# Layer 2's second linear map by seven products of half blocks for groups 4 to 12

## The chip, the cores and the metric

The kernel runs on one core of a Trainium2 chip. Its time is the device time of one execution in microseconds (us). The engines are called by the profile's names: PE is TensorE (PEld its weight loads), DVE is VectorE, ACT is ScalarE, POOL is GpSimd, SP the engine that issues most DMAs. L1089 is line 1089 of the kernel before the change.

## What is computed

Four graph layers run one after the other on x (128 batches of 64 nodes, 256 features, all float32). Each takes a layer norm and a ReLU of x, applies a network with the 64 x 64 adjacency, and adds the result to x. The third of them, called layer 2, is the one that matters here:

```
h   = max(layernorm(x), 0)
agg = A_hat @ h                                     # per batch, over the nodes
h   = relu(batchnorm(agg @ W1.T + b1, g1, be1))     # 256 -> 512
out = batchnorm(h @ W2.T + b2, g2, be2)             # 512 -> 256
x   = x + out
```

The batch norms take mean and variance over all 8192 tokens (batches times nodes), so no value of `out` can be finished before the whole linear map W2 is done. Layer 3 follows with three more linear maps, of which the first takes layer 2's `out`.

## The kernel before

**Groups and buffers.** The 8192 tokens are worked on in 16 groups (NG) of 512 (GN). Inside layer 2 features lie on the partitions: a group's hidden activations are a tile h1s[g] of 128 x 4 x 512, with the 512 hidden features as four chunks of 128, and its output `o` is 128 x 2 x 512. Such tiles are called arenas (L738) and come from three places: ar_right holds eight, ar_left seven, keep one. h1s[0] to h1s[7] lie in ar_right, h1s[8] in keep, the rest in ar_left. The outputs, two groups to an arena, take the arenas of ar_right that the first groups give back. PSUM has eight banks of 128 x 512, handed out in turn (L49).

**The stretch around the change.** The first linear map (hidden_products and hidden_out, L760 to L781) writes h1s and takes a bn_stats of each chunk. bn_finish (L1003) makes scale and shift of the batch norm of it: for each chunk a bn_aggr, an addition, a power on POOL (L1013), and DVE steps of one column (L1016, L1019, L1020). L1016 forms -(mean + bias). For this linear map's norm and the next one's the statistics are taken of the products in PSUM, without the bias, so the bias has to be added to the mean; the stored values have it added as they leave PSUM (L778, and L1098 for the second map).

The loop of L1076 does the second linear map. For each group: four ACT activations in place (L1079: ReLU with the norm's scale and shift), eight matmuls of 128 x 128 weights against 128 x 512 activations (L1089: four chunks of the contraction for each of two output chunks), then for both output chunks a bn_stats (L1103, DVE) and an eviction to `o` with the bias (L1098, ACT). The weights w1 (L949) and w2 (L950) of the two maps are two halves of one tile.

After group 12 (L1106) layer3_weights (L1048) brings layer 3's weights by DMA on SP into arenas that h1s[8] to h1s[11] have given back, and forms sums and differences of their blocks on POOL (L1063 to L1071); some of these go into w1 (L1070). Behind the loop stands bn_finish for the second norm (L1108) and first_start (L1156), the turn into layer 3: normalize, transpose back, add to x, and the first group's layer norm.

**Seven products.** Elsewhere the kernel already multiplies matrices of 2 x 2 blocks with seven products in place of eight (L164 to L237). `sums` forms four combinations of the left matrix's blocks, `differences` four of the right one's, t1 to t4. `seven` issues products 1, 5, 6 and 7 into four banks; ACT copies 1 and 5 out (L173, L174), DVE adds 6 and 7 to these copies (L176, L177). Its function `finish` then has POOL add the two for the block (1, 1) (L180), lets product 2 accumulate on product 1 (block (0, 0), evicted by ACT, L224), product 3 on product 5 and product 4 on product 7 (blocks (0, 1) and (1, 0), added by DVE, L185 and L189). In layer 3 it is used at L1220, L1256 and L1301.

**What sets the order.** The instructions are traced in program order; a planner at compile time then gives each engine its own list, taking by program order what is ready by its own cost estimates, and puts semaphores where an instruction needs another engine's result or a buffer that is still read. Two instructions wait for each other only where the elements that they touch overlap. `tc.issue_after(ins)` keeps a block's instructions behind `ins` on its engine.

Of the kernel before, what the change touches and what calls it, by code (L numbers as in the profile page):

```python
# [9 lines left out]
AF = mybir.ActivationFunctionType  # L10
ALU = mybir.AluOpType
# [3 lines left out]
P = 128  # L15
# [5 lines left out]
NG = NTOK // GN  # L21
# [11 lines left out]
V_B2, V_G2, V_BE2 = 12, 14, 16  # L33
# [5 lines left out]
def adj_preln_kernel(ctx: ExitStack, tc: tile.TileContext, x_in, adj, vec, bg0, bg1,  # L39
                     wg0, wg1, wih, whh, wqkv, w1t, w2t, l3w1, l3w2, l3w3, out):  # L40
    nc = tc.nc
# [7 lines left out]
    def bank(shape=(P, 512)):  # L49
        return psp.tile(list(shape), F32, tag="ps", name="ps")  # L50
# [25 lines left out]
    vecs = const.tile([P, V_N], F32, tag="vecs", name="vecs")  # L76
# [85 lines left out]
    HN = GN // 2  # L162

    def seven(products, banks, p1, p5, out, end, parts=lambda b: [b]):  # L164

        ps = banks  # L170
        for i, p in zip((1, 5, 6, 7), ps):
            products[i](p, True)
        nc.scalar.copy(p1, ps[0])  # L173
        nc.scalar.copy(p5, ps[1])  # L174

        nc.vector.tensor_tensor(p1, p1, ps[2], ALU.add)  # L176
        added = nc.vector.tensor_tensor(p5, p5, ps[3], ALU.add)  # L177

        def finish():
            nc.gpsimd.tensor_tensor(out=out[1][1], in0=p1, in1=p5, op=ALU.add)  # L180
            end(1, 1, None)
            products[2](ps[0], False)
            end(0, 0, ps[0])
            products[3](ps[1], False)
            nc.vector.tensor_tensor(out[0][1], p1, ps[1], ALU.add)  # L185
            end(0, 1, None)
            products[4](ps[3], False)
            for to, p, q in zip(*(parts(b) for b in (out[1][0], p1, ps[3]))):
                last = nc.vector.tensor_tensor(to, p, q, ALU.add)  # L189
                end(1, 0, None, to)  # L190
            return last.ins

        finish.behind = added.ins
        return finish

    def each_behind(behind, i):
        return tc.issue_after(behind[i].ins) if behind else nullcontext()
# [10 lines left out]
    def sums(eng, a11, a12, a21, a22, s1, s2, s3, s4, behind=None):  # L208

        ops = (  # L210
            (s1, a21, a22, ALU.add), (s2, s1, a11, ALU.subtract),
            (s3, a11, a21, ALU.subtract), (s4, a12, s2, ALU.subtract),
        )
        for i, (s, p, q, op) in enumerate(ops):
            with each_behind(behind, i):
                last = eng.tensor_tensor(out=s, in0=p, in1=q, op=op)
        return last.ins

    def ends_in(out, func):


        def end(m, n, ps, part=None):
            if ps is not None:
                nc.scalar.activation(out[m][n], ps, func)  # L224
            elif func != AF.Copy:
                o = out[m][n] if part is None else part
                nc.scalar.activation(o, o, func)  # L227

        return end

    def sevens(w, b, issue):


        (a11, a12), (_, a22), (s1, s2, s3, s4) = w
        (b11, _), (b21, b22), (t1, t2, t3, t4) = b
        pairs = ((a11, b11), (a12, b21), (s4, b22), (a22, t4), (s1, t1), (s2, t2), (s3, t3))
        return {i + 1: issue(*p) for i, p in enumerate(pairs)}  # L237
# [41 lines left out]
    with tc.tile_pool(name="lw", bufs=5) as lw:  # L279
# [6 lines left out]
        with tc.tile_pool(name="gw", bufs=1) as gw, tc.tile_pool(name="gcn", bufs=2) as gp, \  # L286
# [85 lines left out]
            for i, w_d in enumerate((wg0, wg1)):  # L372
                w = gw.tile([P, 2, D], F32, tag=f"wg{i}", name=f"wg{i}")
# [126 lines left out]
        with tc.tile_pool(name="back", bufs=1, reuse_waits="tile") as back_pool, \  # L500
# [188 lines left out]
            for p, nk in ((1, 8), (2, 8), (3, 7), (4, 8)):  # L689
                n = nk * HB  # L690
# [47 lines left out]
    def arena(pool):  # L738
        return pool.tile([P, 4, GN], F32, tag="arena", name="arena")
# [4 lines left out]
    st2 = bp.tile([P, 2, NG, 6], F32, tag="st2", name="st2")  # L744
    h1s = []
# [38 lines left out]
    with tc.tile_pool(name="att", bufs=2, reuse_waits="tile") as ap_:  # L784
# [103 lines left out]
        def attend(eT, v):  # L888
            pss = [bank((P, 2 * GT, NODES)) for _ in range(2)]
            for t in range(GT):  # L890
                for m in range(2):
                    for b in range(2):
                        for par in range(2):
                            rows = slice(par * 64, par * 64 + 64)
                            nc.tensor.matmul(
                                pss[par][b * 64 : b * 64 + 64, 2 * t + m, :],
                                lhsT=eT[rows, 2 * t + m, b * 64 : b * 64 + 64],
                                rhs=v[rows, 2 * t + b, m * 64 : m * 64 + 64],
                                start=True, stop=True,
                            )  # L900
            return pss
# [20 lines left out]
        for g in range(NG):  # L922
            if g == NG - NK + 1:
                hres_pool.__exit__(None, None, None)
                with tc.using_default_side("right"):
                    ar_right = ctx.enter_context(
                        tc.tile_pool(name="arena_r", bufs=NG // 2, reuse_waits="tile")
                    )
            hT_all, blocks = hT
# [5 lines left out]
            q, k, finish = queries_keys(blocks)  # L935
# [11 lines left out]
            if g == NG - 1:  # L947

                w1 = w_att[:, :, 0:512]  # L949
                w2 = w_att[:, :, 512:1024].rearrange("p a (b f) -> a p b f", f=D)  # L950
# [8 lines left out]
            if last is not None:  # L959
                pss = attend(eT, v_last)  # L960
# [22 lines left out]
        with tc.issue_after(sub):  # L983
# [4 lines left out]
            rstd, nmr, _ = ln_scale(xs[2], lambda: add_output(NG - 2, pss, ri))  # L988
# [6 lines left out]
        pss = attend(eT, v_last)  # L995
# [4 lines left out]
    ar_left = ctx.enter_context(tc.tile_pool(name="arena_l", bufs=NG // 2 - 1, reuse_waits="tile"))  # L1000
    outs = []

    def bn_finish(st, n, v_0, v_g, v_b, tag):  # L1003


        scs, shs = [], []
        for m in range(n):
            mv = bp.tile([P, 2], F32, tag=f"{tag}mv{m}", name=f"{tag}mv{m}")
            sc = bp.tile([P, 1], F32, tag=f"{tag}sc{m}", name=f"{tag}sc{m}")
            sh = bp.tile([P, 1], F32, tag=f"{tag}sh{m}", name=f"{tag}sh{m}")  # L1010
            nc.vector.bn_aggr(mv, st[:, m].rearrange("p g s -> p (g s)"))
            nc.vector.tensor_scalar(sc, mv[:, 1:2], BN_EPS, None, ALU.add)
            nc.gpsimd.tensor_tensor(out=sc, in0=sc, in1=mhalf[:, 0:1], op=ALU.pow)  # L1013
            mean = mv[:, 0:1]

            nc.vector.tensor_scalar(  # L1016
                mean, mean, vecs[:, v_0 + m : v_0 + m + 1], -1.0, ALU.add, ALU.mult
            )
            nc.vector.tensor_tensor(sc, sc, vecs[:, v_g + m : v_g + m + 1], ALU.mult)  # L1019
            nc.vector.scalar_tensor_tensor(  # L1020
                sh, mean, sc, vecs[:, v_b + m : v_b + m + 1], ALU.mult, ALU.add
            )
            scs.append(sc)
            shs.append(sh)
        return scs, shs
# [47 lines left out]

    sc1, sh1 = bn_finish(st1, 4, V_B1, V_G1, V_BE1, "n1")

    for g in range(NG):  # L1076
        a = h1s[g]
        for m in range(4):
            nc.scalar.activation(  # L1079
                a[:, m, :], a[:, m, :], AF.Relu,  # L1080
                bias=sh1[m], scale=sc1[m],
            )
        pss = [bank() for _ in range(2)]
        order = [(c, m) for c in range(4) for m in range(2)]
        if g == NG - 1:

            order.sort(key=lambda cm: cm[1])
        for c, m in order:
            nc.tensor.matmul(  # L1089
                pss[m], lhsT=w2[c // 2][:, c % 2, m * P : (m + 1) * P], rhs=a[:, c, :],  # L1090
                start=(c == 0), stop=(c == 3),
            )

        if g % 2 == 0:
            outs.append(arena(ar_right))
        o = outs[-1][:, 2 * (g % 2) : 2 * (g % 2) + 2, :]
        def evicted(m):
            nc.scalar.activation(  # L1098
                o[:, m, :], pss[m], AF.Identity, bias=vecs[:, V_B2 + m : V_B2 + m + 1]
            )  # L1100

        for m in range(2):
            nc.vector.bn_stats(st2[:, m, g, :], pss[m])  # L1103
            if (g, m) != (NG - 1, 1):
                evicted(m)
        if g == NG - 4:  # L1106
            w_three = layer3_weights()
    sc2, sh2 = bn_finish(st2, 2, V_B2, V_G2, V_BE2, "n2")  # L1108

    b1, t1s, a2, s2s, b3, t3s = w_three  # L1110

# [44 lines left out]
    def first_start():  # L1156
# [26 lines left out]
        for g in range(1, 3):  # L1183
            normalize(g, chunks=[1], on_scalar=range(2))
        evicted(1)
        lns = []
        for k in range(2):
# [141 lines left out]
    def finish(g, pss):  # L1329
        if g == NG - 1:  # L1330

            for k in range(2):
                for q, queue in enumerate((nc.sync, nc.scalar)):
                    t = 2 * k + q
                    xt = xs[g][:, t, :]
                    nc.vector.tensor_tensor(xt, xt, pss[q][:, k, :], ALU.add)
                    queue.dma_start(out=out_view[:, g * GT + t, :], in_=xt)
            return
        for q in range(2):
            xq = xs[g].rearrange("p (k q) d -> p q k d", q=2)[:, q]  # L1340
            nc.vector.tensor_tensor(xq, xq, pss[q], ALU.add)
        nc.sync.dma_start(out=out_view[:, g * GT : (g + 1) * GT, :], in_=xs[g])
# [18 lines left out]
    a, finish_start = first_start()  # L1361
    s3 = None
    for g in range(NG + 1):
# [10 lines left out]
        if s3 is not None:  # L1374
            pss = [bank((P, 2, D)) for _ in range(2)]
# [13 lines left out]
        if g < NG:  # L1389
# [6 lines left out]
            if g + 1 < NG:  # L1396
                a = start(g + 1, behind)
# [53 lines left out]
```

## Time and profile before

| | us |
|---|---|
| median of 3 runs | 2474.28 (2473.75 to 2474.61) |
| the profiled execution | 2476.59 |
| its span in the trace | 2474.8 |
| PE busy in the span | 2454.1 |
| the loop of L1076 (1577.6 to 1688.6) | 111.0 |
| PE busy in it | 110.5 |
| DVE, ACT, POOL busy in it | 26.8, 65.6, 21.6 |

Times in the views are counted from the span's start. A line of groups gives the source line, engine and operation, what it writes and reads by the program's tile names, the shape and the count; behind the bar its busy time in us, the mean of one in ns, and the idle time of the engine just before it with what ended most of that. In a timeline the first two numbers are start and duration in us, and the square bracket holds the wait before. A float32 matmul stands as two records. [...]

### The profile page before, as it was taken

The page shows a single profiled execution, that of the slowest core. Times are in us where ns is not written, and L with a number is a line of the kernel's source. Part 1 is how long each engine was busy: PE and PEld are TensorE (multiplying, and loading weights), DVE is VectorE, ACT ScalarE, POOL GpSimd, SP SyncE. Part 2 cuts the span into 40 slices and gives each one's busy share as a digit, 9 for nine tenths or more (in the row PEclk, how much of TensorE's full clock was granted, in tenths as well). Part 3 has the DMA queues.
Part 4 walks back from the last instruction along what each step waited for, and adds up shares of the span by engine and source line. Part 5 has one row for each costly group of instructions (what it writes and reads, how often), then busy time and mean ns, then how long its engine had stood idle before and what let it go on. Part 6 is the DMA issues. An engine that isn't in the chain of part 4 may idle for free.

```text
span 2474.8 us, 46316 instructions
## 1 busy us (share of the span) xinstructions
PE 2454.1 (99%) x19646; PEld 2073.2 (84%) x19646; DVE 1512.6 (61%) x2705; ACT 1145.7 (46%) x2032; POOL 439.8 (18%) x368
## 2 busy tenths in 40 slices
PE   9999999999999999999999999999999999999999
PEld 7678888889999998888888864446998898898888
DVE  6758866666566565566599986425555455454544
ACT  4557754444454443444565566754333323333332
POOL 4432211111111111121133331013011111101110
PEclk9999999999999999999999999999999999999999
DMA  3200000000000000000122110010000000000000
GB/s 126 93 2 1 1 18 1 1 1 34 1 1 1 1 1 1 1 13 1 39 73 71 46 35 1 1 60 1 10 10 18 10 10 16 12 10 10 18 10 18
DMA packets 48558, 48.00 MB, mean 19 GB/s; under 512 B 3680, under 2 KB 44768, under 8 KB 48352
## 3 DMA queue, kind: packets, MB, share of 16 engines
q1 hardware_dynamic: 47360, 44.23, 5.8%
q8 instruction: 154, 2.52, 0.4%
q10 hardware_dynamic: 992, 0.82, 0.1%
q14 instruction: 52, 0.43, 0.1%
HBM read 28.26 MB, written 8.39 MB: 15 GB/s over the span
## 4 chain that ended last, share of the span: by engine, by line
PE 89%; DVE 6%; ACT 2%; issue 1%; POOL 1%; DMA 0%; SPq 0%; ACTq 0%; DVEq 0%; POOLq 0%
PE ps L533 41%; PE ps L1256 16%; PE ps L1301 8%; PE ps L1089 4%; PE ps L766 4%; PE ps L144 4%; PE ps L1220 3%; PE ps L476 2%; PE ps L452 2%; PE ps L799 2%; PE ps L821 1%; ACT arena L227 1%; POOL arena L180 1%; PE ps L882 1%; DVE st L92 0%
## 5 line engine op out<-in xcount | busy, mean ns | idle before, releaser
L533 PE MATMUL ps<-diff,s 128*128 128x256 f32 (+1 forms) x1824 | 393.5, 371 | 0.9 <-DVE diff L653 0.9
L1256 PE MATMUL ps<-arena 128*128 128x256 f32 x1792 | 392.4, 381 | 0.0
L1256 PEld LDWEIGHTS ps<-arena 128*128 128x128 f32 x1792 | 337.9, 190 | 54.0 <-issue 9.3
L533 PEld LDWEIGHTS ps<-diff,s 128*128 128x128 f32 x1824 | 345.9, 190 | 33.8 <-issue 1.6
L547 ACT ACTIVATE gates<-gates,lbias 128x512 f32<-128x512 f32 (+5 forms) x426 | 244.2, 620 | 203.2 <-DVE gates L185 147.3
L180 POOL TENSOR_TENSOR gates<-p 128x512 f32<-128x512 f32 (+1 forms) x115 | 149.6, 1301 | 878.7 <-DVE p L177 827.9
L533 PE MATMUL ps<-h,w 128*128 128x256 f32 (+1 forms) x1028 | 241.0, 371 | 0.0
L533 PE MATMUL ps<-diff,w 128*128 128x256 f32 (+1 forms) x1040 | 238.7, 370 | 0.0
L533 PEld LDWEIGHTS ps<-diff,w 128*128 128x128 f32 x1040 | 197.4, 190 | 18.2
L533 PEld LDWEIGHTS ps<-h,w 128*128 128x128 f32 x1028 | 194.7, 190 | 19.0 <-issue 0.5
L547 ACT ACTIVATE gates<-ps,lbias 128x256 f32<-128x256 f32 (+3 forms) x213 | 91.6, 476 | 247.0 <-PE ps L533 246.9
L227 ACT ACTIVATE arena<-arena 128x512 f32<-128x512 f32 (+1 forms) x160 | 88.6, 582 | 193.4 <-POOL arena L180 101.5
L180 POOL TENSOR_TENSOR arena<-arena 128x512 f32<-128x512 f32 x64 | 73.2, 1143 | 528.4 <-DVE arena L177 528.4
L1301 PE MATMUL ps<-arena 128*128 128x128 f32 x1280 | 149.7, 276 | 0.0
L185 DVE TENSOR_TENSOR gates<-p,ps 128x512 f32<-128x512 f32 (+1 forms) x115 | 76.4, 664 | 119.5 <-PE ps L533 119.4
L1301 PEld LDWEIGHTS ps<-arena 128*128 128x128 f32 x1280 | 145.5, 192 | 1.1
L96 POOL TENSOR_TENSOR rstd<-rstd,mhalf 128x4 f32<-128x4 f32 (+1 forms) x66 | 66.1, 1002 | 425.5 <-DVE rstd L95 418.8
L185 DVE TENSOR_TENSOR arena<-arena,ps 128x512 f32<-128x512 f32 x64 | 39.7, 621 | 152.5 <-PE ps L1256 87.4
L533 PE MATMUL ps<-state,w 128*128 128x256 f32 (+1 forms) x512 | 116.1, 370 | 0.9 <-ACT p L173 0.8
L176 DVE TENSOR_TENSOR p<-p,ps 128x512 f32<-128x512 f32 (+1 forms) x131 | 86.7, 661 | 48.9 <-PE ps L533 48.2
L533 PE MATMUL ps<-state,s 128*128 128x256 f32 (+1 forms) x512 | 115.8, 369 | 0.0
L189 DVE TENSOR_TENSOR gates<-p,ps 128x512 f32<-128x512 f32 (+1 forms) x115 | 76.7, 667 | 63.9 <-PE ps L533 63.2
(185 smaller groups left out, 4063.2 us busy)
## 6 DMA issues: line engine op xcount, KB each, us to landing
x<-in_x SPq DMA_DIRECT2D x27, 512.0 KB, 4.1
v<-vt SPq DMA_DIRECT2D x128, 64.0 KB, 2.1
out<-x SPq DMA_DIRECT2D x15, 512.0 KB, 2.9
w<-in_wih SPq DMA_DIRECT2D x4, 1024.0 KB, 7.5
w<-in_whh SPq DMA_DIRECT2D x3, 1024.0 KB, 4.8
arena<-in_l3w SPq DMA_DIRECT2D x3, 1024.0 KB, 5.2
w<-in_wqkv SPq DMA_DIRECT2D x1, 768.0 KB, 4.4
x<-in_x SPq DMA_DIRECT2D x2, 256.0 KB, 3.2
```

The costliest lines, as they stand in the source:

```text
L144: last = nc.tensor.matmul(pss[b][half * 64 : half * 64 + 64, c, t, :], lhsT=src[rows, t, col : col + 64], rhs=a2[rows, :], start=True, sto ...
L176: nc.vector.tensor_tensor(p1, p1, ps[2], ALU.add)
L180: nc.gpsimd.tensor_tensor(out=out[1][1], in0=p1, in1=p5, op=ALU.add)
L185: nc.vector.tensor_tensor(out[0][1], p1, ps[1], ALU.add)
L189: last = nc.vector.tensor_tensor(to, p, q, ALU.add)
L227: nc.scalar.activation(o, o, func)
L533: nc.tensor.matmul(ps[:, r], lhsT=wc[:, j, :], rhs=bc, start=first and r == 0 and c == 0, stop=True, skip_group_check=True,)
L547: nc.scalar.activation(o, ps, func, bias=lbias[:, col : col + 1])
L766: nc.tensor.matmul(ps, lhsT=w1[:, c, m * P : (m + 1) * P], rhs=a[:, 2 + c, :], start=(c == 0), stop=(c == 1),)
L1089: nc.tensor.matmul(pss[m], lhsT=w2[c // 2][:, c % 2, m * P : (m + 1) * P], rhs=a[:, c, :], start=(c == 0), stop=(c == 3),)
L1256: nc.tensor.matmul(ps[:, r, :], lhsT=w[:, c, col : col + P], rhs=b[:, c, :], start=first and r == 0 and c == 0, stop=c == 1, skip_group_ch ...
L1301: nc.tensor.matmul(ps[:, t, :], lhsT=w[:, c, t * P : (t + 1) * P], rhs=b[:, c, :], start=first and t == 0 and c == 0, stop=c == 3, skip_gr ...
```

## The change

For groups 4 to 12 (SEVEN_FC2) the second linear map is done by `seven`. The left matrix is W2 as 2 x 2 blocks (output chunk m by halves c of the hidden features), the right one the activations as 2 x 2 blocks (halves of the hidden features by halves of the tokens). Each product has 256 tokens and two chunks of contraction. The four sums of weight blocks are made once, on POOL, in w1, which is free by then. The four differences of the activations (128 x 2 x 256 each) go, for each group anew, into one more arena of ar_right, tt, by DVE; the group's activations for this purpose are called for one group ahead. Three of the differences of group g + 1 stand between the first four products of group g and its `finish`, the fourth behind it. Products 1 and 5 are copied into a block of h1s[g] that no product reads. The statistics of these groups read `o` in SBUF, not PSUM.

Groups 0 to 3 and 13 to 15 keep their eight matmuls. All groups now store `o` without the bias b2, and the second norm gets it through its shift: with `biased=False` bn_finish adds the bias to -(mean + bias) again, so that the shift is that of values without it. The diff:

```diff
--- before.py
+++ after.py
@@ -1000,7 +1000,7 @@
     ar_left = ctx.enter_context(tc.tile_pool(name="arena_l", bufs=NG // 2 - 1, reuse_waits="tile"))
     outs = []
 
-    def bn_finish(st, n, v_0, v_g, v_b, tag):
+    def bn_finish(st, n, v_0, v_g, v_b, tag, biased=True):
 
 
         scs, shs = [], []
@@ -1016,6 +1016,8 @@
             nc.vector.tensor_scalar(
                 mean, mean, vecs[:, v_0 + m : v_0 + m + 1], -1.0, ALU.add, ALU.mult
             )
+            if not biased:
+                nc.vector.tensor_tensor(mean, mean, vecs[:, v_0 + m : v_0 + m + 1], ALU.add)
             nc.vector.tensor_tensor(sc, sc, vecs[:, v_g + m : v_g + m + 1], ALU.mult)
             nc.vector.scalar_tensor_tensor(
                 sh, mean, sc, vecs[:, v_b + m : v_b + m + 1], ALU.mult, ALU.add
@@ -1073,39 +1075,101 @@
 
     sc1, sh1 = bn_finish(st1, 4, V_B1, V_G1, V_BE1, "n1")
 
-    for g in range(NG):
+
+
+    SEVEN_FC2 = range(4, NG - 3)
+    fc2_a = [[w2[c][:, :, m * P : (m + 1) * P] for c in range(2)] for m in range(2)]
+
+    fc2_s = [w1[:, :, i * P : (i + 1) * P] for i in range(4)]
+    sums(nc.gpsimd, *fc2_a[0], *fc2_a[1], *fc2_s)
+
+    def fc2_blocks(a):
+        return [
+            [a[:, 2 * c : 2 * c + 2, n * HN : (n + 1) * HN] for n in range(2)] for c in range(2)
+        ]
+
+    def fc2_differences(a, which=range(4)):
+        (b11, b12), (b21, b22) = fc2_blocks(a)
+        t1, t2, t3, t4 = ts
+        ops = ((t1, b12, b11), (t3, b22, b12), (t2, b22, t1), (t4, b21, t2))
+        for i in which:
+            t, p, q = ops[i]
+            nc.vector.tensor_tensor(t, p, q, ALU.subtract)
+
+    def second_linear(a, o):
+
+
+        def product(w, b):
+            def issue(ps, first):
+                for c in range(2):
+                    nc.tensor.matmul(
+                        ps, lhsT=w[:, c, :], rhs=b[:, c, :], start=first and c == 0, stop=c == 1,
+                        skip_group_check=True,
+                    )
+
+            return issue
+
+        blocks = [[o[:, m, n * HN : (n + 1) * HN] for n in range(2)] for m in range(2)]
+        return seven(
+            sevens((*fc2_a, fc2_s), (*fc2_blocks(a), ts), product), [bank((P, HN)) for _ in range(4)],
+            a[:, 0, HN:], a[:, 1, HN:], blocks, ends_in(blocks, AF.Copy),
+        )
+
+    def activate(g):
         a = h1s[g]
         for m in range(4):
             nc.scalar.activation(
                 a[:, m, :], a[:, m, :], AF.Relu,
                 bias=sh1[m], scale=sc1[m],
             )
-        pss = [bank() for _ in range(2)]
-        order = [(c, m) for c in range(4) for m in range(2)]
-        if g == NG - 1:
-
-            order.sort(key=lambda cm: cm[1])
-        for c, m in order:
-            nc.tensor.matmul(
-                pss[m], lhsT=w2[c // 2][:, c % 2, m * P : (m + 1) * P], rhs=a[:, c, :],
-                start=(c == 0), stop=(c == 3),
-            )
+
+    for g in range(NG):
+        a = h1s[g]
+        if g not in SEVEN_FC2:
+            activate(g)
 
         if g % 2 == 0:
             outs.append(arena(ar_right))
         o = outs[-1][:, 2 * (g % 2) : 2 * (g % 2) + 2, :]
-        def evicted(m):
-            nc.scalar.activation(
-                o[:, m, :], pss[m], AF.Identity, bias=vecs[:, V_B2 + m : V_B2 + m + 1]
-            )
-
-        for m in range(2):
-            nc.vector.bn_stats(st2[:, m, g, :], pss[m])
-            if (g, m) != (NG - 1, 1):
-                evicted(m)
+        if g + 1 == SEVEN_FC2[0]:
+            tt = arena(ar_right).rearrange("p i (c n) -> p i c n", c=2)
+            ts = [tt[:, i] for i in range(4)]
+        ahead = g + 1 in SEVEN_FC2
+        if ahead:
+            activate(g + 1)
+        if g in SEVEN_FC2:
+            finish = second_linear(a, o)
+            if ahead:
+                fc2_differences(h1s[g + 1], range(3))
+            finish()
+            if ahead:
+                fc2_differences(h1s[g + 1], [3])
+            for m in range(2):
+                nc.vector.bn_stats(st2[:, m, g, :], o[:, m, :])
+        else:
+            pss = [bank() for _ in range(2)]
+            order = [(c, m) for c in range(4) for m in range(2)]
+            if g == NG - 1:
+
+                order.sort(key=lambda cm: cm[1])
+            for c, m in order:
+                nc.tensor.matmul(
+                    pss[m], lhsT=w2[c // 2][:, c % 2, m * P : (m + 1) * P], rhs=a[:, c, :],
+                    start=(c == 0), stop=(c == 3),
+                )
+
+            def evicted(m):
+                nc.scalar.copy(o[:, m, :], pss[m])
+
+            for m in range(2):
+                nc.vector.bn_stats(st2[:, m, g, :], pss[m])
+                if (g, m) != (NG - 1, 1):
+                    evicted(m)
+            if ahead:
+                fc2_differences(h1s[g + 1])
         if g == NG - 4:
             w_three = layer3_weights()
-    sc2, sh2 = bn_finish(st2, 2, V_B2, V_G2, V_BE2, "n2")
+    sc2, sh2 = bn_finish(st2, 2, V_B2, V_G2, V_BE2, "n2", biased=False)
 
     b1, t1s, a2, s2s, b3, t3s = w_three
 
```

## The prediction

> **What bounds the kernel now.** I read the page first, then the busy time by stage, the groups of instructions inside the stage that is changed, the chain of work that ended last, and the timelines of VectorE and GpSimd. The page's engine shares:
>
> ```profile
> PE 2454.1 (99%) x19646; PEld 2073.2 (84%) x19646; DVE 1512.6 (61%) x2705; ACT 1145.7 (46%) x2032; POOL 439.8 (18%) x368
> ```
>
> TensorE (PE) is busy nearly all the span, but that is an average; the changed loop has to be read by itself. Its groups, from 1577 to 1692 us:
>
> ```profile
> L1089 PE MATMUL ps<-arena,w 128*128 128x512 f32 x256 | 110.5, 593 | 0.5 <-ACT arena L1079 0.5
> ...
> L1079 ACT ACTIVATE arena<-arena,n1sh,n1sc 128x512 f32<-128x512 f32 x62 | 45.2, 819 | 1.9 <-DVE n1sh L1020 1.9
> L1103 DVE BATCH_NORM_STATS2 st<-ps 128x6 f32<-128x512 f32 x32 | 22.4, 698 | 82.4 <-PE ps L1089 82.4
> L1098 ACT ACTIVATE arena<-ps,vecs 128x512 f32<-128x512 f32 x32 | 21.4, 687 | 42.5 <-DVE st L1103 42.1
> ```
>
> The matmuls of line 1089 fill 110.5 of the loop's 111.0 us; VectorE (DVE) works 22.4 us and waits 82.4 us for them. So a microsecond of matmul taken out here comes off the end, as long as nothing else fills its place. The reader should also see x256: 16 groups of 8 matmuls are 256 records, two records a matmul.
>
> The pace is read off VectorE, which starts one statistic for each output as a group ends:
>
> ```profile
> 1591.66 0.70 DVE L1103 BATCH_NORM_STATS2 st<-ps 128x6 f32<-128x512 f32 x1 [5.31 <-PE ps L1089]
> ...
> 1598.53 0.70 DVE L1103 BATCH_NORM_STATS2 st<-ps 128x6 f32<-128x512 f32 x1 [5.31 <-PE ps L1089]
> ```
>
> 1598.53 - 1591.66 = 6.87 us a group, so 6.87/16 = 429.2 ns a record of 512 columns. The pace of 256-column records stands in layer 3's timeline, where seven products already run:
>
> ```profile
> 1712.66 24.34 PE L1256 MATMUL ps<-arena 128*128 128x256 f32 x112
> ```
>
> One record lasts 0.38, so (24.34 - 0.38)/111 = 215.8 ns. The weight load beside it takes 190 ns and fits. A stretch of exactly the new size exists as well: line 1220 issues 28 such records a group, 99.7 us busy over 16 groups, 6.23 us each; 27 x 0.2158 + 0.379 = 6.21. One seven-product block runs there without a gap.
>
> Into the loop leads a chain that TensorE does wait for (pieces of the chain that ended last):
>
> ```profile
> 1574.25 0.56 POOL n1sc L1013
> 1574.84 0.17 DVE n1sc L1019
> 1575.03 0.22 DVE n1sh L1020
> ...
> 1576.75 0.56 POOL n1sc L1013
> ...
> 1582.76 0.82 ACT arena L1079
> ```
>
> Four times a statistic, a power on GpSimd (POOL), two small VectorE steps; the next block's starts behind them. Anything put in it moves the end.
>
> [...]
>
> ```profile
> 622.52 1.45 POOL L180 TENSOR_TENSOR gates<-p 128x448 f32<-128x448 f32 x1 [10.05 <-DVE p L177]
> 623.01 1.44 DVE L654 TENSOR_TENSOR diff<-state,diff 128x448 f32<-128x448 f32 x1
> ```
>
> The same subtraction takes 0.61 us when GpSimd is idle; here it ends 0.48 us after the GpSimd add. [...]
>
> **The change, part by part.**
>
> Matmuls. Removed in each of nine groups: 16 records x 429.2 = 6.867 us. Added: 7 products x 2 chunks x 2 records = 28 x 215.8 = 6.042 us. Gain 0.825 us a group, 9 x 0.825 = **7.42 us**, all on the path.
>
> VectorE in such a group. Four adds of 128x256 (rows of lines 176, 177, 185, 189: 414, 421, 421, 418 ns), four differences of 128x512 (line 205: 690), two statistics (698; from SBUF now, unseen at this width; the 128x256 form of line 92 takes 412, so hardly more). Durations sum to 1.67 + 2.76 + 1.40 = 5.83 us. Neighbours in the queue overlap: three differences in a row took 2.01 us, 0.66 apart; two 128x256 adds 0.75, 0.33 apart; six 128x512 adds 3.67, 0.60 apart. So 1.32 + 2.64 + 1.20 = 5.16. On top comes the lock: GpSimd's new add of the fourth block (128x256, 726 ns, line 180) starts just when the differences do, and holds one of them up by at most 0.73. Bounds 5.16 and 5.83 + 0.73 = 6.56; I take 5.16 + 0.73 = 5.9, under the 6.04 of TensorE. Dates from a group's start: product 7 ends at 3.45 us, the second add by 4.0, then three differences and the lock until 6.7; the next group needs t1 at 6.9, t3 and t2 later (its product 1 needs none), the last difference only at its product 4, 5 us on. The last product of a group waits for the second add: 4.0 against 5.2. TensorE waits for nothing; 0.2 us is the thinnest margin. Allowance for hiccups, such as the four GpSimd differences of layer 3's weights (line 205, 723 ns each) falling in group 9 or 10: 0.1.
>
> ScalarE. Its 64 activations run ahead of the groups (all by 1632 us), so moving group g + 1's ahead costs nothing. Per seven-product group 2 copies and 1 eviction of 128x256 (371, 372, 383) replace two evictions of 687. Product 2 waits for the first copy: 0.86 + 0.2 + 0.37 plus one activation of 0.82 in front = 2.3 us, needed at 3.45. Nothing. If that cover went: a few tenths a group. Evictions without bias cost no more than with it.
>
> The sums of weight blocks on GpSimd: four of 723 ns, 2.9 us, needed 27 us later; but they become ready as group 15's hidden products end (about 1572.6, 1574.3, 1576.0, 1577.8), between GpSimd's powers at 1574.25, 1576.75, 1579.25. A sum in front of a power delays it by up to 0.72; a sum behind it can hold line 1019, which reads two SBUF inputs, for as long. Unseen in this trace: at least 0, at most two or three such meetings, 2.1. I take one: **+0.7**.
>
> The norm's shift: one more one-column VectorE step per chunk (rows of about 160 ns), behind line 1016 and beside GpSimd's power of 0.55 us[...]. 0 to 0.2, I take +0.15 for the last chunk.
>
> Moves: the differences of group 4 are ready during group 3, with VectorE idle 5.31 us of each group; 0 (up to 1.9 if they are queued behind group 3's statistics). No DMA is added, and SP keeps its order; but layer 3's weights come when group 11 lets its buffer go. Before: issue 1661.22, GpSimd's work 1666.76 to 1684.2, the norm's power at 1686.81. After: issue 1661.22 - 8 x 0.825 + 0.7 + 0.6 (the buffer now also waits for the adds) = 1655.9, work ends 1679.0, power wanted at 1680.1. It still fits, by 1.1 us instead of 2.6. The third of these weight blocks now waits for group 12's products, 1660 us, inside this.
>
> Sum: -7.42 + 0.1 + 0.7 + 0.15 = **-6.5 us**. The profiled execution, 2476.59 us (span 2474.8 and 1.8 around it), would become 2470.1 with a span of 2468.3; it stood 2.3 above the median of the runs, so for that 2474.28 - 6.5 = **2467.8 us**.
>
> **Rivals.** *VectorE becomes the bound:* if its steps take their full durations and the lock comes on top, 6.56 us a group; 0.52 over TensorE in 8 following groups is 4.2 us back: 2472.0. For it: 28 records are now little longer than VectorE's list. Against: the overlaps measured above. *GpSimd is late at the turn to layer 3:* its margin of 1.1 us is gone if the blocks start 3 us late (order of the w block, a late landing), about 2 us: 2469.8. Against: the work waits for landing, and that moves with the groups. *Slower: the differences are queued behind the statistics.* The planner places VectorE's list from its own costs. If the three differences land after the last add and both statistics, t1 starts 0.2 + 0.42 + 1.2 after the group's end and is there at 2.5, while the next product 5 wants it at 0.86, and t2 costs TensorE another 0.35: 2.0 us in each of 8 groups, 16 - 6.5, 2483.8. It decides once the stall passes 0.8 us a group. Against: the code puts them ahead of the closing adds, and their inputs are ready 0.2 us after product 7. That the change doesn't do what it says can't be: the products are plain matmuls.
>
> **Chances.** Forecast 0.70 (own range 2466.3 to 2469.2: the entry free, and 0.5 for the spread of runs; or the entry at its worst), VectorE 0.14, GpSimd 0.09, slower 0.07. A measurement tells 0.2%, 5 us, from no change: faster is below 2469.3. Forecast and part of the GpSimd case: 0.74 faster; VectorE and the rest 0.18 the same; 0.08 slower. The range runs from 2466.3 to 2471.5, through the GpSimd case and half of VectorE's; 0.14 is left out.
>
> **What would show it.** Right: 28 records of the new line a group without a gap, groups 5 to 12 ending 6.04 us apart, VectorE idle before its adds on PE, one power or line 1019 in the entry chain late by about 0.6, the first matmul of the turn 6 to 7 us earlier. Wrong: TensorE waiting for VectorE's differences in each group (first or third rival; the third shows statistics ahead of them), GpSimd's power at the end starting straight behind the weight blocks (second), or the entry delayed by over 2 us.

## The result, and the profile after

| | us |
|---|---|
| changed kernel, median of 22 runs | 2470.62 (2469.78 to 2473.02) |
| before, median of 22 runs beside it | 2474.71 (2473.28 to 2476.11) |
| ratio after to before | 0.9985 (95% interval 0.9978 to 0.9991) |
| profiled execution after, its span | 2469.78, 2468.0 |

The kernel became faster by about 4.1 us in the medians, against 6.5 forecast. That is inside the stated range, but above the forecast's own part of it (2466.3 to 2469.2), and above 2469.3, below which the prediction would have called it faster; the interval of the ratio lies clear of 1. The two profiled executions differ by 6.8 us, more than the change is worth: 2.55 us of that arise ahead of the changed loop (from the first matmul to the end of the last hidden product 1576.74 us before, 1574.19 after), where both kernels issue the same instructions but for the first sum of weight blocks on GpSimd. This part varied by 4.3 us over the ten profiles of this study. So the comparison below goes by two stretches that can be read in each of these traces: the **loop**, from the end of the last hidden product (L766) to the first transpose of the turn into layer 3, and the **turn**, from there to layer 3's first product.

| | before | after | difference |
|---|---|---|---|
| loop | 110.74 | 106.54 | -4.20 |
| turn | 10.97 | 10.91 | -0.06 |
| rest, to the end of the span | 775.32 | 775.32 | 0.00 |

The whole change lies in the loop. In the changed kernel line 1105 is a seven-product matmul, 1156 a plain one, 1121 the activation, 1162 the eviction, 1097 a difference, and L1021 is what was L1019. TensorE's timeline through the loop (start, duration, instructions; in brackets the wait ahead of the piece):

```profile
1575.06 1.88 PE L1156 MATMUL ps<-arena,w 128*128 128x512 f32 x4
1577.14 1.98 PE L1156 MATMUL ps<-arena,w 128*128 128x512 f32 x4 [0.20 <-ACT arena L1121]
1580.15 1.99 PE L1156 MATMUL ps<-arena,w 128*128 128x512 f32 x4 [1.02 <-ACT arena L1121]
1582.64 22.58 PE L1156 MATMUL ps<-arena,w 128*128 128x512 f32 x52 [0.51 <-ACT arena L1121]
1605.06 3.62 PE L1105 MATMUL ps<-arena,w 128*128 128x256 f32 x16
1609.99 51.20 PE L1105 MATMUL ps<-arena,w 128*128 128x256 f32 x236 [1.31 <-ACT arena L173]
1661.03 20.76 PE L1156 MATMUL ps<-arena,w 128*128 128x512 f32 x48
```

The reader should see three things. The 236 records of groups 4 (from its product 2 on) to 12 run without a wait: (51.20 - 0.38)/235 = 216 ns from start to start, as forecast. The loop's entry now waits three times, where before it waited once for 0.51. And there is a wait of 1.31 us inside group 4, after its first four products (16 records), for ScalarE's copy L173.

What holds up the entry stands on VectorE. The step n1sc, one column wide, took 0.17 us in the chain that the prediction shows (L1019). After, from VectorE's timeline and then GpSimd's:

```profile
1572.30 0.67 DVE L1021 TENSOR_TENSOR n1sc<-n1sc,vecs 128x1 f32<-128x1 f32 x1 [0.55 <-POOL n1sc L1013]
1575.32 0.67 DVE L1021 TENSOR_TENSOR n1sc<-n1sc,vecs 128x1 f32<-128x1 f32 x1 [0.55 <-POOL n1sc L1013]
...
1581.33 0.16 DVE L1021 TENSOR_TENSOR n1sc<-n1sc,vecs 128x1 f32<-128x1 f32 x1 [0.54 <-POOL n1sc L1013]
```

```profile
1571.70 0.56 POOL L1013 TENSOR_TENSOR n1sc<-n1sc,mhalf 128x1 f32<-128x1 f32 x1 [0.82 <-DVE n1sc L1012]
1572.23 0.72 POOL L216 TENSOR_TENSOR w<-w 128x256 f32<-128x256 f32 x1
```

GpSimd's list has a sum of weight blocks (L216) straight behind each of the first three powers (L1013). The step that needs the power starts beside the sum and ends just after it, at 1572.97. It costs 0.51 us, three times, in a chain where each chunk's statistic stands behind the one before. The fourth power has no sum behind it, and its step takes 0.16.

The wait in group 4 is ScalarE's list:

```profile
1602.26 5.76 ACT L1121 ACTIVATE arena<-arena,n1sh,n1sc 128x512 f32<-128x512 f32 x8
1607.91 0.58 ACT L1162 COPY arena<-ps 128x512 f32<-128x512 f32 x1
1608.38 0.83 ACT L1121 ACTIVATE arena<-arena,n1sh,n1sc 128x512 f32<-128x512 f32 x1
1609.09 0.58 ACT L1162 COPY arena<-ps 128x512 f32<-128x512 f32 x1
1609.56 0.38 ACT L173 COPY arena<-ps 128x256 f32<-128x256 f32 x1
```

Group 4 starts at 1605.06, so its product 1 is done by about 1606.1; the copy of it runs at 1609.56, behind activations of later groups and group 3's late evictions. Product 2 accumulates in the bank that the copy reads, so it can't start earlier. In start-to-start times of TensorE's records the wait costs 1.58 us.

A last, small piece stands at the loop's end: from the start of the last matmul record to the first transpose it is 0.56 us after and 0.49 before, which the norm's shift explains (below). The sum closes: -7.42 of matmuls, +1.57 at the entry (2.54 us over the pace after, 0.97 before), +1.58 in group 4, +0.07 at the end, is -4.20, as measured.

### The profile page after: what moved, and what is told of

Same layout as the page of the kernel before. It is cut to its first block, busy times and chain, and to the rows that moved or that the text cites. A ratio compares the mean times of both kernels' runs of the same rounds, so it can differ in the third digit from the quotient of the medians.

```text
span 2468.0 us, 46700 instructions
## 1 busy us (share of the span) xinstructions
PE 2444.3 (99%) x19754; PEld 2093.1 (85%) x19754; DVE 1549.5 (63%) x2779; ACT 1141.0 (46%) x2041; POOL 452.1 (18%) x381
## 3 DMA queue, kind: packets, MB, share of 16 engines
q8 instruction: 155, 2.54, 0.4%
## 4 chain that ended last, share of the span: by engine, by line
PE 87%; DVE 6%; ACT 4%; DMA 1%; issue 1%; POOL 1%; SPq 0%; DVEq 0%; POOLq 0%; ACTq 0%
PE ps L533 41%; PE ps L1320 16%; PE ps L1365 8%; PE ps L766 4%; PE ps L144 3%; PE ps L1284 3%; PE ps L1105 2%; PE ps L476 2%; PE ps L452 2%; PE ps L799 2%; PE ps L821 1%; ACT arena L1121 1%; PE ps L1156 1%; ACT arena L227 1%; POOL arena L180 1%
## 5 line engine op out<-in xcount | busy, mean ns | idle before, releaser
L180 POOL TENSOR_TENSOR arena<-arena 128x256 f32<-128x256 f32 (+1 forms) x73 | 82.3, 1128 | 589.0 <-DVE arena L177 589.0
L185 DVE TENSOR_TENSOR arena<-arena,ps 128x256 f32<-128x256 f32 (+1 forms) x73 | 43.5, 597 | 157.3 <-PE ps L1320 87.4
```

## The experiments

Each is the changed kernel with one edit. "A" in the expectations is the reading above: the entry's loss is VectorE's step held up beside the sums (0.67 us in place of 0.16), group 4's loss is ScalarE's order; in the two on VectorE's reserve it is that TensorE bounds the groups. Where no median is given there is one run (2469.02 us for the fill, 2473.69 without seven products, 2471.04 from group 8 on, 2470.00 and 2475.34 with one and three more steps). Its time contains the variation ahead of the loop, so it is read by its loop.

**The sums away from the entry.**

```diff
-    sums(nc.gpsimd, *fc2_a[0], *fc2_a[1], *fc2_s)
...
+            if g == 0:
+                with tc.issue_after(counted.ins):
+                    sums(nc.vector, *fc2_a[0], *fc2_a[1], *fc2_s)
```

> The four sums of weight blocks go from GpSimd, beside the entry chain, to VectorE behind group 0's statistics. Loop = from the end of the last hidden product to the first transposes of the turn: 110.74 us before, 106.54 in the changed kernel. Theory A (sums and VectorE's two-input step exclude each other): the three steps n1sc of 0.67 us fall back to 0.16, the loop shortens by 1.5 to 105.0, and the wait of 1.31 us in group 4 stays. Rival B (the entry is late for another reason, the sums only happen beside it): the loop stays at 106.5 within 0.3. Median of the runs: A 2469.1, B 2470.6.

Loop 104.99, median 2468.57 (8 runs), ratio 0.9975 (0.9965 to 0.9985). The entry is the old one again, and the wait in group 4 is still there:

```profile
1608.83 51.20 PE L1104 MATMUL ps<-arena,w 128*128 128x256 f32 x236 [1.32 <-ACT arena L173]
```

VectorE does the four sums in its idle time between the statistics of two groups:

```profile
1572.67 0.16 DVE L1021 TENSOR_TENSOR n1sc<-n1sc,vecs 128x1 f32<-128x1 f32 x1 [0.54 <-POOL n1sc L1013]
...
1584.11 1.54 DVE L216 TENSOR_TENSOR w<-w 128x256 f32<-128x256 f32 x4
1589.50 0.70 DVE L1164 BATCH_NORM_STATS2 st<-ps 128x6 f32<-128x512 f32 x1 [3.85 <-PE ps L1155]
```

**The same places in GpSimd's list, but nothing read.**

```diff
-    sums(nc.gpsimd, *fc2_a[0], *fc2_a[1], *fc2_s)
+    for s in fc2_s:
+        nc.gpsimd.memset(s, 0.001)
```

This kernel leaves the sums out.

> In place of the four sums GpSimd fills the same blocks with a constant: an instruction at the same places of its list that writes SBUF and reads nothing. The sums of weight blocks are left out, so layer 2's values are not the reference's in groups 4 to 12. Theory A (a GpSimd instruction that reads SBUF shuts out VectorE's two-input step): the steps n1sc take 0.16 us, the entry is 1.5 shorter, loop 105.0. Rival E (any GpSimd work beside the chain, or a late power, costs that): n1sc or the powers stay late by 0.5 each, loop 106.5.

Loop 104.96: theory A. The entry is 1.57 us shorter, while the wait in group 4 stays. The fill stands behind the power as the sum did and overlaps the step, which keeps its 0.16 us:

```profile
1573.06 0.31 POOL L1085 MEMSET w<- 128x256 f32 x1
```

```profile
1573.15 0.16 DVE L1021 TENSOR_TENSOR n1sc<-n1sc,vecs 128x1 f32<-128x1 f32 x1 [0.54 <-POOL n1sc L1013]
```

So it is neither that GpSimd is busy nor the order of its list. The fill is shorter than the sum (0.31 against 0.72 us), but the step ends at 1573.31 and the fill at 1573.37: it was not held to the fill's end.

**No seven products at all, the rest kept.** SEVEN_FC2 is empty; the sums on GpSimd, the evictions without bias and the shift stay.

> No group uses seven products; the sums stay on GpSimd (nobody reads them) and the bias stays in the norm's shift. Theory A: the entry costs 1.5, the shift and the evictions without bias nothing: loop 110.74 + 1.54 = 112.3, turn (first transposes to layer 3's first product) 10.9 as before. Rival B (the entry is late because of the seven products' order): loop 110.7. If the shift's step costs what the prediction gave it, the turn is 11.1 instead of 10.9.

Loop 112.37, turn 10.98: the loop is 1.63 us longer than before, without any seven products. By the start times of TensorE's records 1.57 of it is the entry, the cost of the sums, and 0.07 the loop's end, the cost of the shift's extra step.

**ScalarE's copies ahead of later activations.**

```diff
-        if ahead:
+        if ahead and g not in SEVEN_FC2:
             activate(g + 1)
         if g in SEVEN_FC2:
             finish = second_linear(a, o)
+            copied = finish.copied
             if ahead:
+                with tc.issue_after(copied):
+                    activate(g + 1)
```

(`copied` is the second copy in `seven`; the activations of groups 13 to 15 go behind the last such copy too.)

> From group 4 on, ScalarE's activations of a later group are queued behind the second copy of the group that runs; all else as in the changed kernel. Theory A (product 2 of group 4 waits for a copy that stands in ScalarE's list behind activations done too early): the wait of 1.31 us in group 4 falls below 0.2, loop 105.2. Rival B (the first seven-product group has a start-up wait whatever ScalarE's list is): the wait stays above 1 us, loop 106.5. Rival C (activations done only one group ahead come too late): new waits in each group, loop above 107.

Loop 104.97, median 2468.94 (10 runs), ratio 0.9977 (0.9967 to 0.9986). The wait in group 4 is gone and no other has come, though from group 5 on each group's activations are now done only one group ahead:

```profile
1605.41 54.55 PE L1106 MATMUL ps<-arena,w 128*128 128x256 f32 x252
```

In ScalarE's timeline the first two copies follow group 3's evictions at once:

```profile
1606.35 0.59 ACT L1168 COPY arena<-ps 128x512 f32<-128x512 f32 x1 [0.27 <-DVE st L1171]
1606.83 0.38 ACT L173 COPY arena<-ps 128x256 f32<-128x256 f32 x1
1607.39 0.37 ACT L174 COPY arena<-ps 128x256 f32<-128x256 f32 x1 [0.19 <-PE ps L1106]
1607.66 2.93 ACT L1122 ACTIVATE arena<-arena,n1sh,n1sc 128x512 f32<-128x512 f32 x4
```

**Seven products from group 8 on,** `SEVEN_FC2 = range(8, NG - 3)`.

> Seven products for groups 8 to 12 alone, five groups in place of nine; the sums stay on GpSimd. Theory A: the gain is 0.825 us a group, 4.1; the entry costs 1.5 as before; no wait in the first seven-product group, since ScalarE has caught up by group 8: loop 110.74 - 4.13 + 1.54 + 0.1 = 108.2. Rival B (start-up wait of the first such group): a wait of about 1.3 us in group 8, loop 109.5. Rival D (the gain is smaller than 0.825 a group): loop above 108.5 without a wait in group 8.

Loop 108.27, and no wait in group 8:

```profile
1632.20 30.38 PE L1105 MATMUL ps<-arena,w 128*128 128x256 f32 x140
```

The wait is not a start-up cost of the first such group but depends on where ScalarE's list stands (here its last activation is done by 1630), and five groups give five times 0.825: 110.74 + 1.6 - 4.13 = 108.2.

**How much VectorE has left.** The fourth difference is computed twice, and four times:

```diff
-                fc2_differences(h1s[g + 1], [3])
+                fc2_differences(h1s[g + 1], [3, 3])
```

> The fourth difference of a group is computed twice: one more VectorE step of 0.60 us in each of 8 groups. Theory A (TensorE bounds the seven-product groups, VectorE has about 0.76 us idle in each): loop 106.5 to 107.0. Rival C (VectorE already is the bound): 8 x 0.6 = 4.8 more, loop 111.3.

> The fourth difference computed four times: 1.8 us more of VectorE in each of 8 groups. Theory A: the margin of 0.76 us is used up and 1.05 us a group comes to light, 8 x 1.05 = 8.4, loop 114.9. Rival C (VectorE bound before): 8 x 1.8 = 14.4, loop 120.9. If VectorE's margin is larger than read: loop below 112.

Loops 106.91 and 112.04. One more step in each of eight groups costs 0.37 us in all, one short wait in the whole loop; three more cost 5.5 us, less than either theory said. The margin was misread: in the changed kernel groups 5 to 9 leave VectorE 0.8 to 1.0 us each, group 10 only 0.45, but the groups at both ends more. Busy times over the seven-product groups, after and with three more:

```profile
1609.99:1661.03 51.04, 51.04 (x236) 45.02 (x237) 42.64 (x83) 26.16 (x51) 12.39 (x13) 1.00 0.22 73
```

```profile
1610.64:1667.00 56.36, 53.19 (x235) 43.87 (x236) 56.07 (x105) 25.98 (x51) 17.98 (x12) 1.00 0.18 60
```

(stretch; its length, busy PE, PEld, DVE, ACT, POOL with the number of instructions, the granted clock, the DMA share, GB/s.) In the changed kernel VectorE is idle for 51.04 - 42.64 = 8.4 us in all, TensorE never; with three more steps VectorE is busy to the last 0.3 us. 14.4 us of steps less 8.4 of idle is 6.0, near the 5.5 measured. So VectorE was not the bound: 8.4 us are 14 steps of 0.6, not quite two for each of the eight groups.

**Both repairs together.**

> Both edits together. Theory A: the two losses add up, loop 106.54 - 1.5 - 1.3 = 103.7, that is 7.0 below the kernel before, median about 2467.7, ratio about 0.9972. If one of the two hides behind the other: loop 105.0 to 105.2, median 2469.

Loop 103.39, median 2466.67 (5 runs), ratio 0.9967 (0.9955 to 0.9980). All 252 records run without a wait:

```profile
1603.12 54.55 PE L1105 MATMUL ps<-arena,w 128*128 128x256 f32 x252
```

The losses add up, since they lie one after the other on TensorE's path. This is 7.35 us below the loop before: the matmuls alone give 7.42, and the shift's 0.07 is still there. It beats both kernels: its five runs end at 2467.83, and the fastest of the 22 changed ones is 2469.78.

## Why the prediction was right, and where its sizes were off

**Matmuls, -7.42: right.** The record pace is 216 ns in the seven-product groups, and the repaired kernel gets all but the shift's 0.07.

**The entry, +0.7: right in mechanism, wrong in count.** The prediction said that a sum behind a power can hold the two-input step for its length, and took one such meeting. There were three, 0.51 us each, 1.57 together (its bound was 2.1). The first sum ran ahead of the first power and cost nothing; each of the other three stands straight behind a power in GpSimd's list, and straight behind a power is where the held step follows. The prediction counted the chance of a meeting, but the places in the list are fixed: all three sums behind a power met the step. Why the planner set them so was not tried.

**ScalarE, nothing: the step that failed.** It allowed for "one activation of 0.82 in front" of the first copy. When product 1 ended, the rest of a row of eight activations, two late evictions of group 3 and one more activation stood there, 3.4 us of work. Its own premise, that the 64 activations run ahead of the groups, is the cause: ScalarE's list is fixed at compile time, and 39 of the activations stand in it ahead of the first copy, where groups 0 to 4 need 20. ScalarE works them off without a pause from 1581.78 on and is still behind at 1606. The profile of before already had it, in VectorE's and ScalarE's timelines:

```profile
1584.79 0.70 DVE L1103 BATCH_NORM_STATS2 st<-ps 128x6 f32<-128x512 f32 x1 [2.06 <-PE ps L1089]
```

```profile
1582.76 5.74 ACT L1079 ACTIVATE arena<-arena,n1sh,n1sc 128x512 f32<-128x512 f32 x8 [1.10 <-DVE n1sh L1020]
1588.41 1.24 ACT L1098 ACTIVATE arena<-ps,vecs 128x512 f32<-128x512 f32 x2
```

Group 0's first statistic ended at 1585.5, its eviction started at 1588.41, nearly 3 us late. No matmul waited for that eviction, so it looked harmless; in `seven` TensorE waits for what stands at its place. The prediction's price for it, "if that cover went: a few tenths a group", was wrong in kind: TensorE pays once, 1.58 us. The evictions without bias cost no more, as it said: 0.58 us (L1162) against 0.69 (L1098). In group 5 the first copy is still late (1615.29, for a product done by about 1613.6), but it ends before product 2 wants the bank.

**VectorE, nothing: right, but its charge for the lock (GpSimd's add holding up a difference, 0.73 us) was not.** It is not the bound (first rival): in groups 5 to 9 it is busy for 5.1 to 5.3 us, the prediction's sum without the lock (5.16). Only once is a difference held, to 1.18 us at 1643.7 (the others take 0.67 to 0.69), beside layer 3's weight blocks on GpSimd, and TensorE does not wait for it. The add on GpSimd did not hold the differences up; it was held up itself:

```profile
1617.14 1.11 POOL L180 TENSOR_TENSOR arena<-arena 128x256 f32<-128x256 f32 x1 [4.62 <-DVE arena L177]
...
1659.21 0.73 POOL L180 TENSOR_TENSOR arena<-arena 128x256 f32<-128x256 f32 x1 [4.85 <-DVE arena L177]
```

Beside differences it takes 1.04 to 1.12 us, in group 12, where no differences follow, 0.73. The 0.73 that the sum charged to VectorE was GpSimd's to pay, and GpSimd has time (12.39 us busy of 51.04).

**The norm's shift, +0.15: half of it, and elsewhere.** The 0.15 was the author's estimate for a place beside the power. The new step stands behind the one that waits for the power. Before, then after:

```profile
1687.41 0.16 DVE L1019 TENSOR_TENSOR n2sc<-n2sc,vecs 128x1 f32<-128x1 f32 x1 [0.56 <-POOL n2sc L1013]
1687.60 0.22 DVE L1020 SCALAR_TENSOR_TENSOR n2sh<-n2mv,n2sc,vecs 128x1 f32<-128x1 f32 x1
```

```profile
1680.59 0.16 DVE L1021 TENSOR_TENSOR n2sc<-n2sc,vecs 128x1 f32<-128x1 f32 x1 [0.56 <-POOL n2sc L1013]
1680.67 0.15 DVE L1020 TENSOR_TENSOR n2mv<-n2mv,vecs 128x1 f32<-128x1 f32 x1
1680.86 0.22 DVE L1022 SCALAR_TENSOR_TENSOR n2sh<-n2mv,n2sc,vecs 128x1 f32<-128x1 f32 x1
```

The last step starts 0.27 us after the first where it was 0.19, and through one activation the first transpose waits for it: the 0.07 at the loop's end, in the kernel without seven products too. The same step for the second chunk leaves no loss in the turn, which is 10.91 against 10.97.

**The turn to layer 3 (second rival): right.** GpSimd's weight blocks ended at 1678.85 and the norm's power ran at 1679.99, a margin of 1.1 us, as worked out. **The differences behind the statistics (third rival)** did not happen: the planner spread them between the adds and the statistics.

**What of the agreement is luck.** The range reached up to 2471.5 for the first two rivals. Neither happened, so the measured 2470.62 lies where two losses put it that the prediction had too small: 0.7 for 1.57, and nothing for 1.58. Its dates for the profiled execution agree better than its sum deserves: the span 2468.0 for 2468.3 and the end of the weight blocks 1678.85 for 1679.0. There the 2.55 us that this profile was earlier ahead of the loop happen to make up for the 2.2 us by which the sum went too far (-6.5 for -4.26). The first transpose comes 6.75 us earlier, inside the 6 to 7 that the prediction named as a sign of being right, but 2.55 of that, too, arose ahead of the loop.

## What to carry to other kernels

Here the saving came in full where work was taken off the bound engine, and nearly all that was lost was lost where the new stretch begins. Before giving an engine's instruction a waiter, look how late it already runs in the trace of before: an order fixed at compile time can run late without a visible wait, until something waits for it. Preparatory work "needed much later" is not free because its engine is idle: place it behind an event, where no short chain runs on an engine that it can hold up (here 0.51 us at each of three meetings).

## What the runs showed of the hardware

In the changed kernel GpSimd's sum of weight blocks (0.72 us, two inputs from SBUF) held up VectorE's one-column step (two inputs from SBUF) until it ended: the step took 0.67 us in place of 0.16, three times of three. Beside a GpSimd fill of 0.31 us, which reads nothing, it took 0.16. In the pairs shown here the one that started later paid: where VectorE's differences were already running, GpSimd's add took 1.04 to 1.12 us in place of 0.73 and the differences kept their 0.68 to 0.69.
